# Post-norm transformer, two layers: two tiles of the second sequence's probabilities turned by squares instead of on TensorE, and the output bias added in another order

## The chip, the cores and the metric

The kernel runs on one core of a Trainium2 chip. The metric is the device time of one execution in microseconds (us); smaller is better. A core has a matrix engine (TensorE, PE in the profile; its weight loads are PEld), a vector engine (VectorE, DVE), a scalar engine (ScalarE, ACT), GpSimd (POOL) and SyncE (SP), which only issues transfers. They run side by side, each in its own instruction order, and wait for one another by semaphores. SBUF is the on-chip memory; PSUM holds the eight accumulators into which PE writes.

## The reference

Two sequences `b` of 512 tokens with 512 features go through two layers, each an attention and a feed-forward network, with a layer norm after every one of the four:

```python
x = _layernorm(x + _L0_attn_ref(x, ...))   # memory M and normaliser z instead of scores
x = _layernorm(x + _L0_ffn_ref(x, ...))    # ternary weights, int8 in between
x = _layernorm(x + _L1_attn_ref(x, ...))   # softmax(q k^T / sqrt(128)) v, one head, times Wo, plus bo
x = _layernorm(x + _L1_ffn_ref(x, ...))    # silu(x Wg^T) * (x Wu^T), times Wd^T
```

What the change touches is the memory read of the first attention (`num / den` for 8 heads, projected by `Wo`, summed over heads), the test that the first network's weights are ternary, and in the second attention

```python
attn = softmax(q k^T * scale);  out = attn @ v;  return out @ Wo + bo
```

## The kernel before, in words

All work is in tiles of 128 tokens (four a sequence, `NT`) or in blocks of 128 features (four, `NK`). GpSimd executes in the order of the program (L62). For the other engines a scheduler chooses the order; `tc.issue_after(step)` holds an instruction's place behind another's, and the small class `Chain` (L1275 on, `in_turn`) ties a list of steps into a row.

**First attention, reading the memory (L584 to L623, loop at L710).** M and Wo are folded into one 128x512 matrix a head, `mw`, the last column of which gives `den`. For each of eight token tiles `read(b, t)` does eight products `po` on PE (L593), one a head, into a PSUM tile each. ScalarE copies the column `den` (L597), VectorE takes its reciprocal, four heads at a time (L601). The first three heads (`LENT`) are scaled by ScalarE into `y` (L606) and summed on GpSimd (L610, and L622 into the tile `x`); the other five are multiplied and added into `x` by VectorE straight from PSUM (L615), the `steps` of the diff. The layer norm of one tile runs while the next one is read. A tile's PSUM accumulators come free when ScalarE or VectorE has read them.

**The checks (L625, `check_up`).** The first network's gate and up weights come in 11 chunks `gus`, two halves each. For each half ScalarE scales the weights to units (`t`), and VectorE compares that, scaled back, with the weights and counts what differs (`compare`, L211; the count is read out by a small second instruction). Eight of the 22 compares are popped from the list `checks` before the reading starts; the loop at L710 pops six more, two each behind tiles 0 and 1, one each behind 2 and 3, tied to the last fold (`folded`) alone, and the rest follow in the first network. Their sum `tot_up` (L217) and `verdict` follow at tiles 3 and 4.

**Second attention (loop over `b` at L1147, then L1185 to L1310).** Per sequence: queries and keys `pqk` (L1163), values `pv` (L1181), scores `psc` (L1117, PSUM, one 128x512 tile a token tile), the row maximum on VectorE (`maxima`, L1123, a reduction and a small multiplication), and the exponential with its row sum on ScalarE (`exponentials`, L1129). The product with the values needs the probabilities turned (keys on partitions). There are two ways in the kernel:

- on PE: `transposed` (L118) makes sixteen 128x128 transposes into four PSUM tiles and copies each to SBUF (ScalarE and VectorE take turns, L130). The second sequence's probabilities (`pt_p1`, copied to `xt_p1`) are turned so.
- by squares: VectorE turns every 32x32 square of a tile in place of its own (`nc.vector.transpose`, L1195), and `move_squares` (L301) moves the squares to their blocks. With `queues=3`, the default, it issues eight transfers on SyncE and four on GpSimd and leaves four to VectorE as copies (L320); with `queues=2` eight on SyncE and eight on GpSimd. The first sequence's probabilities (`squares_p0`, `pt0`) are turned so.

The output bias `bo` is added to the residual tiles `xs` ahead of time. For the first sequence GpSimd does it in four additions (L1196), in the loop that turns its squares; for the second, GpSimd issues four transfers that add while they write (L1211), behind a small copy `landed` that reads `pt0` (L1209) and so waits until that has been moved. Then `values` (L1221) multiplies values and turned probabilities (`pot`), `output` (L1243) multiplies by Wo (`po1`), `attended` (L1248, the row of L1250) divides by the row sum and adds the residual on VectorE, and `norm_a1` (L1254) normalises: statistics on VectorE, two small steps on GpSimd (L146, L1240), the application on ScalarE (L1241). The first sequence goes through this first, then three tiles of the second; then `turn_rows` (L1286, `pt_f`) turns the first sequence's rows on PE, and the fourth tile of the second sequence follows inside a `Chain`.

**Weights of the second network.** PE multiplies fp32 by parts in a faster format: `split_up` (L1063) cuts a chunk of weights into parts, ScalarE the upper one (`upper`, L1033) and VectorE two more (L1043, L1044), in gaps of the second attention. `table(func, behind)` (L1092) loads ScalarE's table of a function ahead of its first use with a one-element activation; the Silu table is loaded behind the last exponential of the second sequence. The network itself (`up1`, L1353 and L1398; down L1353) follows and takes the rest of the time.

Of the kernel before, what the change touches and what calls it, by code (L numbers as in the profile page):

```python
# [10 lines left out]
F32 = mybir.dt.float32  # L11
# [8 lines left out]
P = 128  # L20
# [19 lines left out]
def kernel(  # L40
# [285 lines left out]
    def pair_tile(name, dtype=F32):  # L326
        return wop.tile([P, 2, HID], dtype, tag="wo", name=name)
# [78 lines left out]
    with tc.tile_pool(name="a0w", bufs=1) as a0w, tc.tile_pool(name="a0", bufs=2) as a0:  # L406
# [303 lines left out]
        for i, (b, t) in enumerate(order):  # L710
            steps = read(b, t, lambda steps: norm_a0(i - 1, steps) if i else None)

            with tc.issue_after(folded.ins):
                for _ in range((2, 2, 1, 1)[i] if i < NT else 0):
                    check_up(*checks.pop(0))
            if i == 3:
                tot_up = total(counts_up[0], "up")
            elif i == 4:
                flag_up, eff_up = verdict(tot_up, sc_up, "up")
            if i == 1:  # L720
                squares0 = xtp.tile([P, NT, HID], F32, tag="xt", name="squares_0")
                xt0 = xtp.tile([P, NT, NK, P], F32, tag="xt", name="xt_f00")
            if 1 <= i <= TURNED:
                turn_squares(i - 1, squares0)
            if i == TURNED:
                move_squares(squares0[:, :TURNED], xt0[:, :TURNED], queues=1)
            if i == NT:
                parts, part, turned = split_tiles(0)
                x2.append(parts)
                part(TURNED, turned(TURNED))  # L730
            elif i == NT + 1:
                squares = xtp.tile([P, NT, HID], F32, tag="xt", name="squares")
                part(NT - 1, turned(NT - 1))
            if NT + 1 <= i <= NT + TURNED:
                with tc.issue_after(steps[0].ins):
                    part(i - NT - 1, xt0[:, i - NT - 1])
            if NT < i < len(order) - 1:
                turn_squares(i - 1, squares)
# [387 lines left out]

        return got, maxima

    def exponentials(b, got, behind={}):  # L1129
        sums = small.tile([P, NT], F32, tag="sums", name=f"sums_{b}")  # L1130
        row = []
        for t, (p, mx) in enumerate(got):
            if t % 2 == 0:
                two = pair_tile(f"prob_{b}_{t}")
            e = two[:, t % 2, :]
            with ExitStack() as tied:
                if t in behind:
                    tied.enter_context(tc.issue_after(behind[t].ins))
                moved = nc.scalar.activation(
                    e, p, AF.Exp, bias=mx, scale=scale, accum_out=sums[:, t : t + 1]  # L1140
                )
            row.append(e)
        probs.append((row, sums))
        return moved

    qkv = []
    for b in range(B):  # L1147
        if b:
            with tc.issue_after(copies[-2].ins), tc.issue_after(copies[-1].ins):
                split_up(0, room0)  # L1150
                split_up(1, room1[:6])
        qk = []
        qk2 = query_tile(f"qk_{b}")
        if b == 0:
            v2 = query_tile("v")
        pqk = [psum(f"pqk_{b}_{j}") for j in range(2)]
        xt = [xt_a11[:, :TURNED], xt_a11[:, TURNED:]] if b else xt_a10
        for half in (1, 0) if b else (0, 1):
            for j in range(2):
                for k in range(NK):  # L1160
                    p = pqk[j].rearrange("p (h t i) -> p h t i", h=2, i=P)[:, half]
                    rows = xt[half][:, :, k, :]
                    nc.tensor.matmul(  # L1163
                        p, wqkv[:, k, ts(j, D)], rows,
                        start=(k == 0), stop=(k == NK - 1),
                    )
        for j, p in enumerate(pqk):
            s = qk2[:, j, :]
            moved = nc.scalar.activation(s, p, AF.Identity, bias=bqk[:, j : j + 1])
            qk.append(s)  # L1170
        if b:
            pt0 = fp.tile([P, NT, NK, P], F32, tag="it10", name="pt_p0", bufs=1)
            move_squares(squares, pt0)
            pt0 = pt0.rearrange("p t k i -> p k t i")
        else:
            table(AF.Exp, moved)
        v = v2[:, b, :].rearrange("p (t d) -> p t d", t=NT)
        for t in range(NT):
            p = psum(f"pv_{b}_{t}")
            for k in range(NK):  # L1180
                nc.tensor.matmul(  # L1181
                    p[:, :D],
                    xt[t // TURNED][:, t % TURNED, k, :],
                    wqkv[:, k, ts(2, D)],
                    start=(k == 0), stop=(k == NK - 1),  # L1185
                )
            nc.vector.tensor_add(v[:, t, :], bv, p[:, :D])
        qkv.append((qk[0], qk[1], v))
        if b == 0:
            got, maxima = scores(0, turn_others)  # L1190
            maxima(range(NT))
            exponentials(0, got)
            squares = fp.tile([P, NT, HID], F32, tag="it00", name="squares_p0", bufs=1)
            for t in range(NT):
                nc.vector.transpose(squares[:, t, :], probs[0][0][t])  # L1195
                nc.gpsimd.tensor_add(xs[0][t], xs[0][t], bo)  # L1196


    room2 = room1[6:] + take(4)
# [2 lines left out]
            weight_upper(gus[turn[2]][:, a].rearrange("p k i -> p (k i)"), room2[3 * a])  # L1202

    got, maxima = scores(1)
    scaled_max = maxima(range(NT))
    table(AF.Silu, exponentials(1, got))

    landed = small.tile([P, 1], F32, tag="off", name="landed")
    nc.gpsimd.tensor_copy(landed[2 * SQ : 3 * SQ], pt0[2 * SQ : 3 * SQ, NK - 1, NT - 1, P - 1 :])  # L1209
    for t in range(NT):  # L1210
        nc.gpsimd.dma_start(xs[1][t], bo_in.to_broadcast([P, HID]), accum_op=ALU.add)  # L1211
    with tc.issue_after(scaled_max.ins):
        done = split_up(2, room2, True)
    with tc.issue_after(done.ins):
# [6 lines left out]
    def values(b, pt, cuts):  # L1221

        ot = ot2[:, b, :]
        w = S // cuts
        for i in range(cuts):
            po = psum(f"pot_{b}_{i}")
            for k in range(NT):
                nc.tensor.matmul(  # L1228
                    po[:, :w].rearrange("p (t i) -> p t i", i=P), qkv[b][2][:, k, :],
                    pt[:, k, ts(i, NT // cuts)],  # L1230
                    start=(k == 0), stop=(k == NT - 1),
                )
            (nc.vector.tensor_copy if b else nc.scalar.copy)(ot[:, ts(i, w)], po[:, :w])
        ots.append(ot)
# [8 lines left out]
    def output(b, t):  # L1243
        p = psum(f"po1_{b}_{t}")
        nc.tensor.matmul(p, ots[b][:, ts(t, P)], wo1, start=True, stop=True)  # L1245
        return p
# [52 lines left out]
        return pts, turned  # L1299

    values(0, pt0, 1)
    pt1 = transposed(probs[1][0], "p1").rearrange("p k (t i) -> p k t i", t=NT)
    for t in range(NT):
        attended(0, t, output(0, t))
        norm_a1(0, t)
    values(1, pt1, 2)
    for t in range(NT - 1):
        done = attended(1, t, output(1, t))
    rooms = [rows_room(0, "r0"), None]
    x3 = [row_blocks(rooms[0]), None]  # L1310
    pts, turned = turn_rows(0)
    with tc.issue_after(turned.ins):
        p = output(1, NT - 1)
    in_turn = Chain(done)
    for pt, (h, m, _) in zip(pts, x3[0]):
        in_turn(lambda: upper_lower(pt, h, m)[1])
    for t in range(NT - 1):
        in_turn(lambda: norm_a1(1, t))
    in_turn(lambda: attended(1, NT - 1, p))
    x = xs[1][NT - 1]  # L1320
    stats = layernorm_stats(x, f"a11_{NT - 1}")
    in_turn.last = taken[f"a11_{NT - 1}"]
    squares = xtp.tile([P, NT, HID], F32, tag="xt", name="squares_r1")
    for t in range(NT - 1):
        in_turn(lambda: nc.vector.transpose(squares[:, t, :], xs[1][t]))
    in_turn(lambda: layernorm_apply(x, x, stats))
    in_turn(lambda: nc.vector.transpose(squares[:, NT - 1, :], x))
    for h, m, d in x3[0]:
        in_turn(lambda: crossed(d, h, m))
    xt_r1 = fp.tile([P, NT, NK, P], F32, tag="it10", name="xt_f11", bufs=1)  # L1330
# [233 lines left out]
    for i, (b, j) in enumerate(steps):  # L1564
# [6 lines left out]
            while len(held) > 1:  # L1571
                moved = finish_up()
        if i == 1:
            in_turn(lambda: split_up(AHEAD - 1, take(6)))
        elif i == 2:
            rooms[1] = rows_room(1, "r1")
            x3[1] = row_blocks(rooms[1])
            for k in range(NK):
                with tc.issue_after(in_turn.last.ins):
                    uppers, in_turn.last = rows_from_squares(k)  # L1580

            landed = small.tile([P, 1], F32, tag="off", name="landed_r1")
            nc.gpsimd.tensor_copy(landed[:SQ], x3[1][NK - 1][0][:SQ, S - 1 :].bitcast(F32))
            gus[2:6] = up_weights(gu1_in, "1", range(2, 6), nc.gpsimd)
            wds = down_weights(wd1_in, "1", nc.gpsimd)
        elif i == AHEAD:
            for h, m, d in x3[1]:
                in_turn(lambda: crossed(d, h, m))
# [85 lines left out]
```

## Time and profile before

| what | value |
| --- | --- |
| time, median of 3 runs | 453.56 us (452.8 to 453.66) |
| the profiled execution's own time | 453.97 us |
| its span, first to last instruction | 452.2 us |
| mean granted TensorE clock | 0.999 |
| instructions | 5904 |
| packets of transfers, bytes | 37220, 38.97 MB |
| sixteen engines for transfers, share of the span used by the hardware queue / the software queue | 18.5% / 10.9% |
| memory read of the first attention, `po` L593, 128 PE records | 57.2 us busy, 599 ns each |
| VectorE's sums of it, L615, 40 | 29.8 us, 746 ns each |
| GpSimd's sums of `y`, L610, 16 | 21.3 us, 1332 ns each |
| the sixteen transposes of the second sequence's probabilities on PE, L128 | records of 273 ns that overlap, starting from 254.7 to 256.3 |

The page gives, for each engine, how long it was busy and what share of the span that is; then the span in 40 slices; the queues of the transfers; the chain of work that ended last, followed back from the end; and the costliest groups of instructions, each with its line, engine, operation, the tile that it writes and those that it reads, the count, the busy time, and the idle time just before with what ended it. In a timeline of an engine a row is: start in us, busy us, engine, line, operation, tiles, shapes, count, and in brackets how long the engine had idled before and which instruction it then followed ("0.50 <-PE pt_p L128"). Equal instructions that follow one another stand in one row, with the sum of their time.

### The profile page before, as it was taken

How to read it: one execution, taken by the hardware profiler on the slowest of the kernel's cores; microseconds unless marked ns; L12 is line 12 of the kernel's file. 1: busy time of each engine (PE TensorE's matmuls, PEld its weight loads, DVE VectorE, ACT ScalarE, POOL GpSimd, SP SyncE). 2: the span in 40 equal slices, each digit the busy share in tenths (PEclk: the TensorE clock that was granted, in tenths of full speed). 3: DMA queues.
4: the chain of work that ended last, by engine and by line, in shares of the span. 5: the costliest groups of instructions: out<-in, count | busy, mean ns of one | idle time of the engine just before them, and what ended most of it. 6: DMA issues, size and time to landing. Idle time of an engine off the chain costs nothing.

```text
span 452.2 us, 5904 instructions
## 1 busy us (share of the span) xinstructions
PE 444.8 (98%) x1921; PEld 338.9 (75%) x1921; DVE 317.7 (70%) x638; ACT 259.6 (57%) x494; POOL 127.8 (28%) x184
## 2 busy tenths in 40 slices
PE   8999999999999999999999999999999999999995
PEld 8887753444587888888878578888888888888885
DVE  4976657877886798858899999545535446777523
ACT  5788986467566975557745645454645446442311
POOL 0200205566650049302465347350000000011211
PEclk9999999999999999999999999999999999999999
DMA  8999990020028101121216603390000000000001
GB/s 297 396 268 318 169 331 6 0 44 7 1 46 238 42 2 48 48 94 39 34 33 160 101 1 53 83 393 3 0 1 0 1 2 0 1 18 29 34 37 70
DMA packets 37220, 38.97 MB, mean 86 GB/s; under 512 B 25264, under 2 KB 26160, under 8 KB 37184
## 3 DMA queue, kind: packets, MB, share of 16 engines
q1 hardware_dynamic: 32960, 26.66, 18.5%
q0 software_dynamic: 3936, 11.47, 10.9%
q8 instruction: 22, 0.36, 0.3%
q10 hardware_dynamic: 288, 0.36, 0.2%
q14 instruction: 14, 0.11, 0.1%
HBM read 32.45 MB, written 2.10 MB: 76 GB/s over the span
## 4 chain that ended last, share of the span: by engine, by line
PE 95%; ACT 2%; DMA 1%; DVE 1%; issue 0%; DVEq 0%; ACTq 0%
PE pu L1353 24%; PE pd L1353 13%; PE po L593 10%; PE pg_f L789 9%; PE pq L538 9%; PE pu_f L789 9%; PE pd_f L848 4%; PE pqk L1163 3%; PE pu L1398 2%; PE pv L1181 2%; PE pot L1228 2%; PE psc L1117 2%; PE po L1245 2%; DMA gu<-in_gu 1%; PE pmw L579 1%; PE pq L509 1%
## 5 line engine op out<-in xcount | busy, mean ns | idle before, releaser
L593 PE MATMUL po<-mw,q 128*128 128x512 f32 x128 | 57.2, 599 | 0.7 <-ACT y L606 0.6
L146 POOL TENSOR_TENSOR rstd_f<-mv_f,ln_eps 128x1 f32<-128x1 f32 x15 | 6.4, 428 | 163.2 <-DVE mv_f L1521 128.1
L1353 PE MATMUL pu<-r,ugu 128*128 128x512 f32 x200 | 48.6, 389 | 0.0
L364 ACT ACTIVATE pu<-pu 128x512 f32<-128x512 f32 x42 | 24.2, 581 | 41.3 <-PE pu L1353 37.6
L593 PEld LDWEIGHTS po<-mw,q 128*128 128x128 f32 x128 | 22.7, 189 | 33.6 <-issue 17.2
L1353 PEld LDWEIGHTS pu<-r,ugu 128*128 128x128 f32 x200 | 37.5, 188 | 7.8
L615 DVE SCALAR_TENSOR_TENSOR x<-po,den,x 128x511 f32<-128x511 f32 x40 | 29.8, 746 | 1.9
L170 ACT ACTIVATE ta_f<-y_f,below_half 128x512 int8<-128x512 f32 (+1 forms) x22 | 15.9, 722 | 24.6 <-DVE y_f L158 22.2
L610 POOL TENSOR_TENSOR y<-y,y 128x511 f32<-128x511 f32 x16 | 21.3, 1332 | 24.0 <-DVE x L615 20.3
L1412 DVE TENSOR_TENSOR it_f<-ev,pu 128x512 f32<-128x512 f32 x20 | 13.7, 685 | 16.0 <-PE pu L1353 15.6
L1353 PE MATMUL pu<-r,it_early 128*128 128x512 f32 x104 | 24.9, 389 | 0.0
L1241 ACT ACTIVATE x<-x,off_f,rstd_f 128x512 f32<-128x512 f32 x7 | 5.7, 815 | 32.0 <-POOL off_f L1240 32.0
L815 DVE SCALAR_TENSOR_TENSOR it_f<-tb_f,ta_f 128x512 fp32r<-128x512 int16 (+1 forms) x22 | 15.6, 707 | 11.1 <-ACT tb_f L171 11.1
L1353 PEld LDWEIGHTS pu<-r,it_early 128*128 128x128 f32 x104 | 19.5, 188 | 4.1
L1353 PE MATMUL pd<-ugu,r 128*128 128x512 f32 (+1 forms) x79 | 22.5, 362 | 0.0
L789 PE MATMUL pg_f<-x,tu 128*128 128x512 f32 x88 | 22.1, 393 | 0.0
L789 PE MATMUL pu_f<-x,tu 128*128 128x512 f32 x88 | 21.7, 389 | 0.0
L376 POOL TENSOR_SCALAR td<-wd,inv_down 128x512 fp32r<-128x512 f32 x11 | 19.9, 1824 | 3.2 <-DVE inv_down L206 3.2
L848 PE MATMUL pd_f<-td,it_f 128*128 128x512 f32 x88 | 20.3, 389 | 0.0
L597 ACT ACTIVATE den<-po,den_eps 128x1 f32<-128x1 f32 x64 | 14.0, 270 | 10.6 <-PE po L593 10.5
L789 PEld LDWEIGHTS pg_f<-x,tu 128*128 128x128 f32 x88 | 16.4, 188 | 4.0 <-DVE x L615 0.4
L789 PEld LDWEIGHTS pu_f<-x,tu 128*128 128x128 f32 x88 | 16.5, 188 | 3.4
(400 smaller groups left out, 1129.3 us busy)
## 6 DMA issues: line engine op xcount, KB each, us to landing
gu<-in_gu SPq DMA_DIRECT2D x16, 512.0 KB, 5.3
wo<-in_wo SPq DMA_DIRECT2D x8, 512.0 KB, 9.5
wo<-in_wo POOLq DMA_DIRECT2D x8, 512.0 KB, 9.1
wd<-in_wd SPq DMA_DIRECT2D x10, 256.0 KB, 5.4
wd<-in_wd POOLq DMA_DIRECT2D x10, 256.0 KB, 6.6
wq<-in_wq SPq DMA_DIRECT2D x8, 256.0 KB, 4.7
gu<-in_gu POOLq DMA_DIRECT2D x4, 512.0 KB, 5.1
x<-in_x SPq DMA_DIRECT2D x7, 256.0 KB, 4.3
```

The lines of the kernel that those rows point to most:

```text
L170: nc.scalar.activation(a[:n], y, AF.Relu, bias=below_half[:n])
L364: return nc.scalar.activation(p, p, AF.Copy, scale=BIG + 1.0)
L376: eng.tensor_scalar(out, w, factor, None, ALU.mult)
L538: done = nc.tensor.matmul(p, w, x, start=(start and i == 0), stop=(i == len(todo) - 1), skip_group_check=not start,)
L593: nc.tensor.matmul(po, qs[b][h0 + j][:, ts(t, P)], mw[:, h0 + j, :], start=True, stop=True,)
L597: nc.scalar.activation(den[:, j : j + 1], po[:, LAST:], AF.Identity, bias=den_eps)
L610: nc.gpsimd.tensor_add(ys[0][:, :LAST], ys[0][:, :LAST], y[:, :LAST])
L615: steps.append(nc.vector.scalar_tensor_tensor(x[:, :LAST], four[j][:, :LAST], d, x[:, :LAST], ALU.mult, ALU.add))
L789: nc.tensor.matmul(pp[a], t[:, a, i % NK, :], x2[b][i], start=(i == 0), stop=(i == 2 * NK - 1),)
L815: nc.vector.scalar_tensor_tensor(it[:n], tb[:n], 128.0, ta[:n], ALU.min, ALU.subtract)
L848: nc.tensor.matmul(pd, inter[b][c][:, ts(t, P)], td[c].bitcast(F32R), start=(c == 0), stop=(c == last),)
L1353: done = nc.tensor.matmul(p, w, x, start=(start and i == 0), stop=(i == n - 1), skip_group_check=not start,)
```

## The change

Three edits.

1. The late checks are tied to the first VectorE sum of the tile behind which they are popped, besides the last fold.
2. Of the second sequence's probabilities tiles 0 and 1 (`TURNED` = 2) are turned by squares, with eight transfers on SyncE and eight on GpSimd, each half as large as with four tiles; tiles 2 and 3 stay on PE, eight transposes instead of sixteen, now into a PSUM tile per token tile. VectorE's turns stand between the maxima, and the exponentials are split accordingly. The product `pot` of the second sequence takes its halves in reverse order, the token tiles that come last in the chain are chosen so that tile 1 is the last instead of tile 3, and the Silu table load and a later weight split are tied behind the copy of tile 2.
3. The bias transfers to the second sequence's residual tiles take the place of the additions in the first sequence's loop, and the additions for the first sequence stand where the transfers were, ahead of the eight transfers that GpSimd issues for edit 2. The copy `landed` is gone.

```diff
@@ loop at L710
-            with tc.issue_after(folded.ins):
+            with tc.issue_after(folded.ins), tc.issue_after(steps[0].ins):
                 for _ in range((2, 2, 1, 1)[i] if i < NT else 0):
                     check_up(*checks.pop(0))
@@ exponentials, L1129
-    def exponentials(b, got, behind={}):
...
+    def exponentials(b, got, tiles=range(NT)):
+        if 0 in tiles:
+            pairs = [pair_tile(f"prob_{b}_{t}") for t in range(0, NT, 2)]
+            sums = small.tile([P, NT], F32, tag="sums", name=f"sums_{b}")
+            probs.append(([u for two in pairs for u in units(two)], sums))
+        row, sums = probs[b]
+        for t in tiles:
+            p, mx = got[t]
+            moved = nc.scalar.activation(
+                row[t], p, AF.Exp, bias=mx, scale=scale, accum_out=sums[:, t : t + 1]
+            )
         return moved
@@ loop over b, b == 0, L1194
             for t in range(NT):
                 nc.vector.transpose(squares[:, t, :], probs[0][0][t])
-                nc.gpsimd.tensor_add(xs[0][t], xs[0][t], bo)
+                nc.gpsimd.dma_start(xs[1][t], bo_in.to_broadcast([P, HID]), accum_op=ALU.add)
@@ behind the loop, L1204
     got, maxima = scores(1)
-    scaled_max = maxima(range(NT))
-    table(AF.Silu, exponentials(1, got))
-
-    landed = small.tile([P, 1], F32, tag="off", name="landed")
-    nc.gpsimd.tensor_copy(landed[2 * SQ : 3 * SQ], pt0[2 * SQ : 3 * SQ, NK - 1, NT - 1, P - 1 :])
+    squares1 = fp.tile([P, NT, HID], F32, tag="it00", name="squares_p1", bufs=1)
+    pt1 = xtp.tile([P, NT, NK, P], F32, tag="xt", name="xt_p1")
+    scaled_max = maxima(range(TURNED))
+    exponentials(1, got, range(TURNED))
+    for t in range(TURNED):
+        turned = nc.vector.transpose(squares1[:, t, :], probs[1][0][t])
+        with tc.issue_after(turned.ins):
+            scaled_max = maxima([TURNED + t])
+        exponentials(1, got, [TURNED + t])
     for t in range(NT):
-        nc.gpsimd.dma_start(xs[1][t], bo_in.to_broadcast([P, HID]), accum_op=ALU.add)
+        nc.gpsimd.tensor_add(xs[0][t], xs[0][t], bo)
+    move_squares(squares1[:, :TURNED], pt1[:, :TURNED], queues=2)
     with tc.issue_after(scaled_max.ins):
         done = split_up(2, room2, True)
@@ values
-        for i in range(cuts):
+        for i in reversed(range(cuts)):
@@ behind values(0, pt0, 1)
-    pt1 = transposed(probs[1][0], "p1").rearrange("p k (t i) -> p k t i", t=NT)
+    for t in range(TURNED, NT):
+        pt = psum(f"pt_p1_{t}")
+        for k in range(NK):
+            nc.tensor.transpose(pt[:, ts(k, P)], probs[1][0][t][:, ts(k, P)], ident)
+        move = nc.vector.tensor_copy if t % 2 else nc.scalar.copy
+        moved = move(pt1[:, t], pt.rearrange("p (k i) -> p k i", k=NK))
+        if t % 2 == 0:
+            table(AF.Silu, moved)
+            settled = moved
+    pt1 = pt1.rearrange("p t k i -> p k t i")
...
-    for t in range(NT - 1):
+
+    *others, final = [*range(TURNED, NT), *range(TURNED)]
+    for t in others:
         done = attended(1, t, output(1, t))
...
@@ second network, steps
         if i == 1:
-            in_turn(lambda: split_up(AHEAD - 1, take(6)))
+            with tc.issue_after(settled.ins):
+                in_turn(lambda: split_up(AHEAD - 1, take(6)))
```

Where the diff is cut behind `others`, every `range(NT - 1)` of the old text has become `others` and every `NT - 1` has become `final`.

More of the change, by code (lines that the diff above doesn't have):

```diff
@@ L1127, in scores @@
         return got, maxima
-    def exponentials(b, got, behind={}):
[L1130 to L1143, printed above, removed]
+    def exponentials(b, got, tiles=range(NT)):
[9 more added lines that the diff above has]
+            )
         return moved
@@ L1312 @@
     with tc.issue_after(turned.ins):
-        p = output(1, NT - 1)
+        p = output(1, final)
     in_turn = Chain(done)
@@ L1316 @@
         in_turn(lambda: upper_lower(pt, h, m)[1])
-    for t in range(NT - 1):
+    for t in others:
         in_turn(lambda: norm_a1(1, t))
[L1319 to L1322, printed above, removed]
+    in_turn(lambda: attended(1, final, p))
+    x = xs[1][final]
+    stats = layernorm_stats(x, f"a11_{final}")
+    in_turn.last = taken[f"a11_{final}"]
     squares = xtp.tile([P, NT, HID], F32, tag="xt", name="squares_r1")
-    for t in range(NT - 1):
+    for t in others:
         in_turn(lambda: nc.vector.transpose(squares[:, t, :], xs[1][t]))
     in_turn(lambda: layernorm_apply(x, x, stats))
-    in_turn(lambda: nc.vector.transpose(squares[:, NT - 1, :], x))
+    in_turn(lambda: nc.vector.transpose(squares[:, final, :], x))
     for h, m, d in x3[0]:
```

## The prediction

> **What bounds the kernel now.** I read the page's busy rows and chain of waits first, then the chain in order of time, then the timelines of the two stages that the diff touches.
>
> ```profile
> span 452.2 us, 5904 instructions
> PE 444.8 (98%) x1921; PEld 338.9 (75%) x1921; DVE 317.7 (70%) x638; ACT 259.6 (57%) x494; POOL 127.8 (28%) x184
> ...
> PE 95%; ACT 2%; DMA 1%; DVE 1%; issue 0%; DVEq 0%; ACTq 0%
> ```
>
> PE ends last nearly everywhere, so an edit counts only by how far it moves PE. The chain in order of time leaves PE in one long stretch, 59.32 to 73.24, where the reading of the first token tile starts; from there to 446.86 it is PE alone. But PE without idle time can still be paced: an operand that is ready just in time is invisible in the chain, and becomes the limit when it moves. I therefore follow VectorE (DVE) too.
>
> **Edit 1, the late checks (L713).** Six compares (L211) stood ahead of the first tile's sums; now two stand behind the first sum of tile 0, two in tile 1, one each in tiles 2 and 3. VectorE's timeline:
>
> ```profile
> 70.68 1.56 DVE L211 SCALAR_TENSOR_TENSOR junk<-t,sc_up,gu 128x512 int8<-128x512 f32 x1
> 72.17 0.08 DVE L211 DVE_READ_ACCUMULATOR junk<-t,sc_up,gu 128x1 f32 x1
> 72.17 0.17 DVE L601 RECIPROCAL den<-den 128x4 f32<-128x4 f32 x1
> 72.28 0.17 DVE L217 TENSOR_REDUCE tot_up<-counts 128x1 f32<-128x14 f32 x1
> 72.44 3.31 DVE L615 SCALAR_TENSOR_TENSOR x<-po,den,x 128x511 f32<-128x511 f32 x4
> 75.67 0.17 DVE L601 RECIPROCAL den<-den 128x4 f32<-128x4 f32 x1
> 75.94 0.75 DVE L615 SCALAR_TENSOR_TENSOR x<-po,den,x 128x511 f32<-128x511 f32 x1
> 78.37 0.18 DVE L601 RECIPROCAL den<-den 128x4 f32<-128x4 f32 x1 [1.68 <-ACT den L597]
> ```
>
> The reciprocal at 72.17 waited behind a compare. Its last input came from ScalarE at 71.09 (70.79 + 0.30), and in the new order of ScalarE I count it to 70.95. So the four sums move up about 1.1 us and free PSUM for PE that much sooner. What is late next: the two compares of tile 1 (0.75 each and 0.08 for reading the count, 1.66) go into the hole of 1.68 before 78.37. They would just fit, but GpSimd's additions (L622, L610, 1.27 each) run there, and 70.68 above shows what that does: 1.56 instead of 0.75 beside such an addition. With sums 1.1 earlier, L622 runs from 74.75 and L610 from 76.13; the first compare, due at 75.47, waits to 75.88, the second to about 77.6, and the reciprocal comes at 78.33 instead of 78.37. The gain is then given back to 0.04. Nothing restores it: the sums of a tile, the reciprocal, ScalarE's three scaled copies and the next sums form a loop of 7.3 us a tile (sums end at 82.36 and 89.69), against 6.9 of PE. The compares of tiles 2 and 3 have holes of 1.62 and 1.47 for 0.83. Bounds 0 to 1.1; I take **-0.2**, near the blocked row.
>
> **Edit 2, two tiles turned in squares.** PE does 8 transposes fewer: 16 take 1.75 in the chain, so -0.88. The copy of `ot` (L1233) stood behind the Silu table load, its warm-up and an `ugu` copy (1.28 + 0.20 + 0.61) and started at 255.42; with those moved behind it, it can start when pot ends (254.83), so PE's next product (po, 256.42) can come at about 255.7. But VectorE carries the next step. Timeline now:
>
> ```profile
> 249.44 0.69 DVE L1123 TENSOR_REDUCE mx<-psc 128x1 f32<-128x512 f32 x1
> ...
> 255.75 0.69 DVE L130 COPY xt_p<-pt_p 128x512 f32<-128x512 f32 x1 [0.50 <-PE pt_p L128]
> 256.62 0.69 DVE L130 COPY xt_p<-pt_p 128x512 f32<-128x512 f32 x1 [0.18 <-PE pt_p L128]
> 257.55 0.75 DVE L1250 SCALAR_TENSOR_TENSOR x<-po,sums,x 128x512 f32<-128x512 f32 x1 [0.23 <-PE po L1245]
> ```
>
> Added between the maxima: two turns (0.71 and 0.65 in the rows of L1195), 1.35 with the waits for their exponentials. Gone: one copy (0.69) and the idle 0.91. The first sum at 257.55 moves by -0.25. From there VectorE is dense to 263.93, and the fourth tile's norm ends on ScalarE at 266.06 (265.25 + 0.81); PE's first block of pt_f (265.88) takes that tile in its fourth transpose, so end of pt_f = that norm + 1.5 = 267.6, against 267.8 in the chain. **Slack 0.2: behind it, every us on VectorE is a us on PE.**
>
> The sixteen transfers of `xt_p`: SyncE issues eight at 0.66 and GpSimd eight at 0.6, 5.3 us from the second turn, and they land 1.9 later (row xt_a). The turn ends at 253.1 without delays, so 260.3; the reversed halves use them last, after four po and half of pot, at 260.9 by my count. Hidden, by 0.6; the issues on GpSimd also end before its first norm step (now 259.92). On SyncE nothing waits behind.
>
> **Edit 3, bias transfers and sums change places.** This is the term that decides. GpSimd now adds from 245.68 to about 250.6, just behind its pt_p issues, where VectorE has, back to back:
>
> ```profile
> 243.09 2.57 POOL L316 DMA_DIRECT2D pt_p<-squares_p  x4 [2.07 <-DVE squares_p L1195]
> ...
> 245.70 0.68 DVE L1043 SCALAR_TENSOR_TENSOR it_early<-it_early,gu 128x512 fp32r<-128x512 f32 x1
> 246.30 0.41 DVE L320 COPY pt_p<-squares_p 32x512 f32<-32x512 f32 x1
> 246.63 0.67 DVE L1044 TENSOR_TENSOR it_early<-it_early,it_early 128x512 fp32r<-128x512 f32 x1
> 247.32 1.29 DVE L320 COPY pt_p<-squares_p 32x512 f32<-32x512 f32 x3
> ```
>
> What an addition there does is seen where it stands today, and in the stages before:
>
> ```profile
> 236.06 4.97 POOL L1196 TENSOR_TENSOR x<-x,bo 128x512 f32<-128x512 f32 x4
> 240.49 1.09 DVE L1043 SCALAR_TENSOR_TENSOR it_early<-it_early,gu 128x512 fp32r<-128x512 f32 x1
> 98.53 0.94 DVE L233 TENSOR_SCALAR eff_up<-sc_up,yes_up,no_up 128x2 f32<-128x2 f32 x1
> 402.28 1.40 POOL L146 TENSOR_TENSOR rstd_f<-mv_f,ln_eps 128x1 f32<-128x1 f32 x1 [96.74 <-DVE mv_f L1521]
> ```
>
> L1043 took 1.09, not 0.68: it ran on only when the additions ended at 241.03. L233, with one SBUF tensor as input, took 0.94 (0.27 at 171.35). An L290 at 113.92 took 1.49, not 0.42, beside L610: 1.07 is what one addition costs whoever waits from its start. The turns (0.71) and the maxima (0.68, from PSUM) in the same stretch lost nothing, so only VectorE work from SBUF is hit. The last row is the other side: GpSimd's 0.19 waited 1.2 us through three VectorE operations, each issued before the one ahead ended. Without a gap VectorE mostly goes first; with one, the waiting addition does (69.98: between two compares). In the stretch above, the three copies from 247.32 stand 0.013 apart, issued after the one ahead has ended: three gaps, and a waiting addition each.
>
> No row shows a copy L320 beside an addition. Bounds: nothing, if VectorE keeps its turn; four additions, 4 x 1.07 = 4.3. Nearest are L233 (one SBUF input, blocked) and the gap at 69.98; I take three, 3 x 1.07 = 3.2. Less the 0.41 that L1043 loses today at 240.49: **+2.8 on VectorE**. The first sum moves by 2.8 - 0.25 = 2.55, pt_f by 2.55 - 0.2 = **+2.3 on PE**. PE's saved 0.88 is idle time then.
>
> The Trainium skill's "SBUF — State Buffer", section "SBUF: two separate sides", speaks against this edit: it calls the port pair shared by VectorE and GpSimd an exclusive lock, held for a whole instruction, and counts an fp32 copy from SBUF to SBUF among those that take it. The blocked rows agree. By its "whole instruction" four additions would cost 4 x 1.27 = 5.1 on VectorE and the sum would be 1.9 higher, an estimate; by rows for two-input operations alone it would be the first rival.
>
> The bias transfers (3.64 of issues at 250.26, 6.1 to land) start at 236.1 in place of the additions (4.97), so GpSimd is free before the turn at 242.8 as now; they are needed at 264.37. The `landed` copy (0.18) costs nothing. `settled`, the order of halves and of `final` keep all counts.
>
> **Sum** against the profiled execution: 453.97 (452.2 and 1.8 around it) - 0.2 + 2.3 = 456.1; it is 0.41 above the median of 453.56, so **455.7** on the median's footing.
>
> **Rivals.** (a) One addition gets in, in the idle port time between L1043 and L1044, and the copies pass: 1.07 - 0.41 - 0.25 - 0.2 = +0.2, less 0.2: 453.6. For it: no row has a copy blocked. (b) The other side: VectorE stays ahead of all four additions, as in the row of 402.28. VectorE gains 0.41 + 0.25, PE 0.86; with 0.2 to 1.1 of edit 1 that is 452.5 to 451.6, say 452.0. It decides from fewer than one addition before the maximum at 249.44. (c) The bias transfers, now with the gu loads (two of 512 KB at 236.9) and ahead of pt_p, make pt_p late: PE's pot (LDWEIGHTS at 250.81) and the first turn (it overwrites what pt_p reads) wait. The DMA row is busy some 7 us for the biases (252 to 259.5), 3.3 for gu, 4.3 for pt_p; one after another from 237.8 they end at 252.6, 1.5 late for the turn at 251.15: 454.4 without any blocking. Against it: pt_p is spread over 5 us by its issues anyway.
>
> **Chances.** Forecast 0.50, its own range 454.6 (two additions) to 456.8 (four); (a) 0.18; (b) 0.24; (c) 0.08. Faster by over 0.2% (0.9 us, about what a measurement tells from no change) is (b), 0.24; within it (a) and part of (c), 0.21; slower 0.55. The range 452.0 to 456.9 leaves out half of (b) and a tail above.
>
> **What would show it.** Right: rows of L320 and L1043 near 246 longer by about 1.1, the maximum of the second sequence 2 to 4 us later behind its pv, ScalarE's fourth norm as PE's releaser before pt_f, additions of 1.3 to 2 us; the reciprocal of tile 1 near 78.3. Wrong: L320 at 0.42 beside the additions; po straight behind eight transposes; pot waiting for a transfer, which is (c).

## The result, and the profile after

The changed kernel takes 458.56 us (median of 5 runs, 457.61 to 459.0) against 453.61 for the kernel before: a ratio of 1.0109, 95% interval 1.0097 to 1.012. It is 4.95 us slower; the forecast was 455.7, and the range up to 456.9 does not hold it. The profiled execution took 457.61.

From the page of the changed kernel, the counterpart of the rows shown of before:

```profile
span 455.8 us, 5910 instructions
PE 446.3 (98%) x1913; PEld 338.7 (74%) x1913; DVE 323.5 (71%) x639; ACT 259.4 (57%) x493; POOL 131.9 (29%) x191
...
PE 90%; DVE 7%; ACT 1%; issue 1%; POOL 0%; ACTq 0%; DVEq 0%; POOLq 0%
```

PE is still 98% busy, with eight instructions fewer. But VectorE now holds 7% of the chain that ended last, where it had 1%: a stretch in which PE follows VectorE. VectorE's timeline of the changed kernel shows where:

```profile
242.93 6.79 DVE L1044 TENSOR_TENSOR it_early<-it_early 128x512 fp32r<-128x512 f32 x2
...
250.24 0.41 DVE L320 COPY pt_p<-squares_p 32x512 f32<-32x512 f32 x1
...
253.37 0.68 DVE L1123 TENSOR_REDUCE mx<-psc 128x1 f32<-128x512 f32 x1
```

Before, the same two stood in VectorE's timeline as

```profile
244.50 1.28 DVE L1044 TENSOR_TENSOR it_early<-it_early 128x512 fp32r<-128x512 f32 x2
```

And GpSimd's, in the same stretch of the changed kernel:

```profile
241.53 2.67 POOL L316 DMA_DIRECT2D pt_p<-squares_p  x4 [2.97 <-DVE squares_p L1191]
244.22 4.95 POOL L1211 TENSOR_TENSOR x<-x,bo 128x512 f32<-128x512 f32 x4
```

Two L1044 took 6.79 instead of 1.28, 5.5 more, and they end 0.55 after the fourth addition: **one VectorE instruction, the second L1044 (6.19), waited for all four additions**. Everything behind it is as long as it was, the copies L320 too (0.41), and comes later. The first row maximum of the second sequence stands at 253.37, and PE, done with the scores, waits for VectorE to read the values out of a PSUM tile (L1183; waits of the changed kernel: us, times, longest):

```profile
PE pot L1229 <- DVE v L1183: 2.7, 1, 2.7
```

To compare kernels whose earlier stages differ by some tenths, I use one length from PE's timeline: from the end of the second sequence's `pv` to the end of `pt_f`. It is 19.82 in the kernel before and 24.66 in the changed one, +4.84, nearly the whole loss of 4.95.

### The profile page after: what moved, and what is told of

Same layout as the page of the kernel before. It is cut to its first block, busy times and chain, and to the rows that moved or that the text cites. A ratio compares the mean times of both kernels' runs of the same rounds, so it can differ in the third digit from the quotient of the medians.

```text
span 455.8 us, 5910 instructions
## 1 busy us (share of the span) xinstructions
PE 446.3 (98%) x1913; PEld 338.7 (74%) x1913; DVE 323.5 (71%) x639; ACT 259.4 (57%) x493; POOL 131.9 (29%) x191
## 4 chain that ended last, share of the span: by engine, by line
PE 90%; DVE 7%; ACT 1%; issue 1%; POOL 0%; ACTq 0%; DVEq 0%; POOLq 0%
PE pu L1365 23%; PE pd L1365 13%; PE po L593 12%; PE pq L538 9%; PE pg_f L789 9%; PE pu_f L789 9%; PE pd_f L848 4%; DVE it_early L1044 2%; PE pu L1410 2%; PE po L1246 2%; PE pmw L579 2%; PE pq L509 1%; PE pot L1229 1%; PE ph L1365 1%; PE rise L113 1%; PE pdc L1365 1%
## 5 line engine op out<-in xcount | busy, mean ns | idle before, releaser
L146 POOL TENSOR_TENSOR rstd_f<-mv_f,ln_eps 128x1 f32<-128x1 f32 x15 | 5.4, 359 | 163.9 <-DVE mv_f L1533 128.8
L848 PEld LDWEIGHTS pd_f<-td,it_f 128*128 128x128 f32 x88 | 16.5, 188 | 3.4
```

Of the source, the lines that this page charges most:

```text
L848: nc.tensor.matmul(pd, inter[b][c][:, ts(t, P)], td[c].bitcast(F32R), start=(c == 0), stop=(c == last),)
```

## The experiments

Theory: the loss is VectorE held up by the four additions, for their whole row. Rivals: the transfers (the bias ahead of `pt_p`, or `xt_p` by itself) do it, and the additions only cover that; or an addition slows VectorE wherever it stands. Each kernel is compared with runs of the kernel before on the same chip.

| kernel | median us | ratio to before, 95% | end of pv to end of pt_f |
| --- | --- | --- | --- |
| before | 453.6 to 454.1 | | 19.82 |
| edit 1 alone | 453.52 | 0.9999 (0.999 to 1.0008) | 19.83 |
| edit 3 undone | 458.2 | 1.0103 (1.0084 to 1.0121) | 22.41 |
| edit 3 alone | 458.39 | 1.0104 (1.0089 to 1.0119) | 24.62 |
| sums by transfer | 461.17 | 1.0165 (1.0151 to 1.0179) | 27.99 |
| a pause behind each sum | 459.77 | 1.013 (1.0103 to 1.0156) | 24.93 |
| no sums | 453.62 | 0.9994 (0.9982 to 1.0006) | 19.74 |
| edit 2, no bias transfers | 453.29 | 0.9993 (0.9979 to 1.0007) | 20.47 |
| bias transfers last | 455.26 | 1.0049 (1.0026 to 1.0072) | 21.27 |
| sums beside the maxima | 454.08 | 1.0003 (0.9991 to 1.0015) | 20.31 |
| two sums | 455.97 | 1.0038 (1.0024 to 1.0052) | 22.21 |

The last column is of the one profiled execution of each, the others of all runs (with the pauses, of three out of four).

**Edit 1 alone.** The kernel before with

```diff
-            with tc.issue_after(folded.ins):
+            with tc.issue_after(folded.ins), tc.issue_after(steps[0].ins):
```

> The kernel before with edit 1 alone. Theory from the trace of after: the six compares kept the first reciprocal, and behind it ScalarE's scaled copies, back by 1.9 us, PE stood idle for it, and nothing takes that back: 453.6 - 1.3 = 452.3. Rival, the step as recorded in the prediction: only the second reciprocal moves, and the compares of tile 1 give it back: 453.6 - 0.2 = 453.4.

Measured: 453.52. The interval is 0.45 below to 0.36 above the kernel before: my theory of 1.3 from the two profiles falls, and the prediction's 0.2 can't be told from nothing. The two profiles had the reading, from the first `po` to the first `pg_f`, at 58.32 before and 57.06 after, and PE's idle 0.57 and 0.17 in it gone. But edit 3 alone, which has the old order of the checks, needs 57.30, with no idle time of PE, and edit 1 alone 57.04. What was different in the profiled execution of before is one row of ScalarE's timeline:

```profile
65.14 0.72 ACT L374 ACTIVATE tu<-gu,inv_up 128x512 fp32r<-128x512 f32 x1 [0.92 <-DMA gu<-in_gu]
```

The same row in the kernel with edit 3 alone:

```profile
64.78 0.72 ACT L374 ACTIVATE tu<-gu,inv_up 128x512 fp32r<-128x512 f32 x1
```

In that execution of the kernel before the weights landed late under the reading, and the six compares could not start. It is not the only one: ScalarE waits 0.60, 0.51 and 0.21 for them in the profiles of two sums, of no sums and of the sums beside the maxima, which all have edit 1, and there the reading takes 57.76, 57.65 and 57.37. So late weights lengthen the reading in the new order as in the old; where they land in time, the two orders are 0.26 apart in one profile each. The profiled execution of the changed kernel also began its reading early, at 61.79, where the ten experiments begin at 62.1 to 62.6; that would account for most of the 0.95 that it took less than its median.

**Edit 3 undone** (edits 1 and 2 stay, and `landed` is back ahead of the second loop).

```diff
-                nc.gpsimd.dma_start(xs[1][t], bo_in.to_broadcast([P, HID]), accum_op=ALU.add)
+                nc.gpsimd.tensor_add(xs[0][t], xs[0][t], bo)
...
-        nc.gpsimd.tensor_add(xs[0][t], xs[0][t], bo)
+        nc.gpsimd.dma_start(xs[1][t], bo_in.to_broadcast([P, HID]), accum_op=ALU.add)
```

> After with edit 3 undone: the four additions in the first sequence's loop, the copy landed and the bias transfers ahead of the transfers of xt_p; edits 1 and 2 stay. Theory (all of the loss is the additions holding VectorE up): 453.6 - 1.3 (edit 1) - 0.45 (edit 2, the 0.25 and 0.2 of the prediction) = 451.9, and the parts of the weights at 243 to 250 run at 0.6 to 0.7 us each. Rival (turning two tiles by squares costs by itself, by the turns between the maxima or late transfers): above 454.

Measured: 458.2, with runs from 456.12 to 459.49, against a theory of 451.9. VectorE is free of waits, as the theory has it (two L1044 in 1.28), yet the time is not won. GpSimd's timeline, and then the waits, of this kernel:

```profile
249.83 3.65 POOL L1213 DMA_DIRECT2D x<-in_bo  x4 [0.33 <-issue]
253.32 3.69 POOL L316 DMA_DIRECT2D xt_p<-squares_p  x6
```

```profile
PE pot L1231 <- DMA xt_p<-squares_p: 3.1, 1, 3.1
```

The bias transfers are issued ahead of `xt_p` and are in flight beside them; those of `xt_p` take 6.0 us to land, not 1.9 to 2.6 as in the kernels where no bias transfer is beside them, and GpSimd's last two issues wait 1.10 and 1.43 for a bias transfer. So edits 2 and 3 hang together: with the old places of the bias, edit 2 costs some 4.6; with the new ones, the additions cost 4.9. The profile explains 2.6 of the 4.6 (22.41 against 19.82): it is of the fastest of the six runs, and what the others wait for is open.

**Edit 3 alone.** The kernel before with the bias transfers in the first sequence's loop, the additions behind `scores(1)`, and no `landed`.

> The kernel before with edit 3 alone. Theory: the four additions, one behind another without a gap, hold VectorE up for their whole time, 5.5 us for one L1044, less 0.4 saved, less 0.2 of slack: 453.6 + 4.9 = 458.5. Rival 1, the recorded step (three of four additions get in, 1.07 each): 456.2. Rival 2 (the loss needs the turns and transfers of edit 2): 453.6.

Measured: 458.39, the theory's 458.5. VectorE's timeline:

```profile
243.73 6.78 DVE L1044 TENSOR_TENSOR it_early<-it_early 128x512 fp32r<-128x512 f32 x2
```

The two L1044 take as long without edit 2, to 0.01 us.

**Sums by transfer.** The changed kernel with

```diff
-        nc.gpsimd.tensor_add(xs[0][t], xs[0][t], bo)
+        nc.gpsimd.dma_start(xs[0][t], bo_in.to_broadcast([P, HID]), accum_op=ALU.add)
```

> After, with the four additions on GpSimd replaced by four accumulating transfers of the bias in the same place. Theory (the shared port): no VectorE operation is stretched, 451.9 as with edit 3 undone. Rival (the bias transfers, early or many, delay the transfers of the probabilities): above 455, with pot waiting for a transfer.

Measured: 461.17, against a theory of 451.9. No VectorE row is stretched, but the rival's mechanism is there in full:

```profile
PE pot L1229 <- DMA pt_p<-squares_p: 5.8, 1, 5.8
```

Eight bias transfers around `pt_p` hold it up until 256.7. This kernel therefore says nothing on the additions; it shows that the transfers are a second brake as soon as there are more of them.

**No sums.** The changed kernel without the four additions.

```diff
-        nc.gpsimd.tensor_add(xs[0][t], xs[0][t], bo)
```

> After without the four additions: the first sequence's output bias is left out; the bias transfers of the second stay where they are. Theory (the additions carry the loss; the early bias transfers let the transfers of pt_p land at about 250 to 251, some 1 us later than before but just in time): 453.6 - 0.45 + 0.2 = 453.3. Rival 1 (the early bias transfers are a second brake of the same size behind the additions): 455 to 457, with pot or the first turn of the second sequence waiting for pt_p. Rival 2 (the transfers of xt_p come late once nothing else is): 455 to 457, with the second product pot waiting for xt_p.

Measured: 453.62, the time of before. The additions carry the loss. The transfers of `pt_p` take 5.5 us to land in the changed kernel (2.4 on SyncE's queue and 2.8 on GpSimd's before), but without the additions `pot` starts at 251.40, 0.33 behind the last score, and the length to the end of `pt_f` is 19.74: the delay is hidden. The two L1044 take 1.28 again, beside the same four issues of GpSimd.

**Two sums.** The changed kernel with additions for two tiles.

```diff
-    for t in range(NT):
+    for t in range(2):
         nc.gpsimd.tensor_add(xs[0][t], xs[0][t], bo)
```

> After with two of the four additions (the output bias of two tiles of the first sequence is left out). Theory (VectorE waits from 0.6 us ahead of the first addition to the end of the last, whatever their number): L1044 takes about 3.7 us instead of 6.2, the time lies half way between none (453.6) and four (458.6), at 456.1 to 456.4. Rival (the loss is a threshold: it comes only when PE runs idle for so long that its clock falls): 454 or less, or 458 and more.

Measured: 455.97, a little under the theory's 456.1: 1.9 more than before, and in the profile 2.47 more than with none (22.21 against 19.74), half of the 4.92 for four. VectorE's timeline:

```profile
243.99 4.35 DVE L1044 TENSOR_TENSOR it_early<-it_early 128x512 fp32r<-128x512 f32 x2
```

4.35 - 1.28 = 3.07 for a row of additions of 2.51; with four it was 5.51 for 4.95. Both times the wait is the row's length and 0.56.

**A pause behind each sum.** The changed kernel with

```diff
         nc.gpsimd.tensor_add(xs[0][t], xs[0][t], bo)
+        pause = small.tile([P, 1], F32, tag="off", name=f"pause_{t}")
+        nc.gpsimd.tensor_copy(pause[:1], xs[0][t][:1, :1])
```

> After, with a one-element copy on GpSimd behind each of the four additions, which reads what the addition wrote, so that no two additions follow one another without a pause. Theory A (whichever engine holds the port keeps it as long as its instructions follow one another without a pause): VectorE gets in behind the first addition, L1044 takes about 2 us instead of 6.2; the other three additions come in at the pauses between the copies of L320, and the time stays between 456.5 and 458.6. Rival B (GpSimd goes first whatever stands between): L1044 over 6 us, 458.6 or more.

Measured: 459.77, the median of 458.49, 459.77 and 460.06; one execution of 1173.77 is left aside, and its cause is not known. VectorE's timeline, then GpSimd's:

```profile
243.55 3.13 DVE L1044 TENSOR_TENSOR it_early<-it_early 128x512 fp32r<-128x512 f32 x2
246.60 1.89 DVE L1043 SCALAR_TENSOR_TENSOR it_early<-it_early,gu 128x512 fp32r<-128x512 f32 x1
248.41 1.62 DVE L320 COPY pt_p<-squares_p 32x512 f32<-32x512 f32 x1
```

```profile
244.84 1.28 POOL L1211 TENSOR_TENSOR x<-x,bo 128x512 f32<-128x512 f32 x1
246.18 0.54 POOL L1213 COPY pause<-x 1x1 f32<-1x1 f32 x1
```

At each pause VectorE gets one instruction in (the second L1044 takes 2.53 and ends at 246.67, beside the small copy), and then it waits for the next addition: 1.85, 1.21, 1.21 and 1.12 (the three L320, 2.40 for 1.28), 5.39 in all. Half of theory A holds: a row of additions without a pause gives nothing away, a pause does. The other half falls: VectorE's own row without a pause was broken: from the second L1044 on, four of five instructions waited. The copies L320 from SBUF to SBUF wait as well, 1.62 and 1.53 instead of 0.41. The sum in the profile stays the same. Rival B falls on L1044, for which it had over 6 us, though the time lies in its range; that the other two runs took 1.3 to 1.6 more than the profiled one is not explained.

**Edit 2 without bias transfers** (edits 1 and 2, additions in the loop as before).

> Edits 1 and 2 with the additions in the first sequence's loop as before and without any bias transfer: the second sequence's output bias is left out. Prices edit 2 without its neighbours. The prediction's step: 453.6 - 0.45 - 0 (edit 1 alone measured at nothing) = 453.1, xt_p landing at about 260 and pot not waiting for it. Rival (the sixteen transfers of xt_p are late by themselves): above 454.5, with pot waiting for xt_p.

Measured: 453.29 against 453.70 for before, no difference that the interval shows. The first sum on VectorE comes at 256.88, 0.29 earlier than with edit 1 alone. In the profile PE waits 1.1 for `xt_p`; but that execution took 454.17, 0.88 more than the median. In the profiles of no sums, of the bias transfers last and of the sums beside the maxima PE does not wait for `xt_p`: the cover holds mostly, not always.

**Bias transfers last** (as the one before, with the transfers issued behind those of `xt_p`).

> Edits 1 and 2, additions in the first sequence's loop as before, and the bias transfers of the second sequence issued behind those of xt_p, in the order in which the tiles are used. Theory: xt_p is alone on the transfer engines until about 260, the bias lands from 262 to 267, in time but for the last tiles: 453.1 to 454.2. Rival (the sums of the second sequence wait for their bias): 455 or more, with a wait of attended for x.

Measured: 455.26. `xt_p` is in time, but four more issues on GpSimd hold the norms behind them: ScalarE's first norm starts at 262.70 instead of 260.40, and `pt_f` waits for the last. The rival's wait for the bias is there too, 0.71 ahead of one sum (L1251 at 265.41), but the chain that ended last runs through the queue of GpSimd, which neither theory had. The profile is of the fastest of ten runs, which go up to 459.08.

**Sums beside the maxima.** The changed kernel with the additions behind the first maximum of the second sequence.

```diff
+    behind = small.tile([P, 1], F32, tag="off", name="behind")
+    nc.gpsimd.tensor_copy(behind, got[0][1])
     for t in range(NT):
         nc.gpsimd.tensor_add(xs[0][t], xs[0][t], bo)
```

> After, with a one-column copy on GpSimd ahead of the four additions that reads the second sequence's first row maximum, so that the additions run from about 250 to 255, beside VectorE's maxima (from PSUM) and turns. Theory (only VectorE work with its tensors in SBUF is held up; the place of the additions decides): the maxima and turns keep 0.65 to 0.71 us, the L1043 behind them (253.8) waits about 1.1, the transfers of xt_p start 1.7 later and pot waits for them by about 1: 454.6 to 455.6. Rival (additions on GpSimd hold VectorE up wherever they stand): 457.5 or more, with maxima of 1 us and longer.

Measured: 454.08 against 454.10 for before, better than expected. GpSimd's row, then VectorE's:

```profile
249.89 4.95 POOL L1213 TENSOR_TENSOR x<-x,bo 128x512 f32<-128x512 f32 x4
```

```profile
249.60 0.68 DVE L1123 TENSOR_REDUCE mx<-psc 128x1 f32<-128x512 f32 x1
...
252.03 0.65 DVE L1123 TENSOR_REDUCE mx<-psc 128x1 f32<-128x512 f32 x1
252.61 0.69 DVE L1206 STREAM_TRANSPOSE squares_p<-prob 128x512 f32<-128x512 f32 x1
...
254.04 1.35 DVE L1043 SCALAR_TENSOR_TENSOR it_early<-it_early,gu 128x512 fp32r<-128x512 f32 x1
```

The same four additions, as long as before, cost nothing beside maxima and turns; the one L1043 that starts under them waits 0.67. The place decides, and these two lines take back the whole loss. No kernel tried is measurably faster than the one before.

## Why the prediction was wrong, step by step

The direction, the stretch and the edit were right: edit 3, VectorE behind the issues of `pt_p`, PE late by what VectorE is late. The sum was 2.9 too small: 2.3 of that is one term, 0.2 the slack, and up to 0.2 edit 1.

- **The step that failed: "I take three, 3 x 1.07 = 3.2", and its upper bound, "four additions, 4 x 1.07 = 4.3".** Measured: 5.5, one wait for all four. The price came from rows where an addition was followed by a pause, and so did the picture that a waiting VectorE instruction gets in between two additions: the two additions at 69.98 depend on one another, and the second starts 0.08 after the first has ended (71.76 and 71.68). The four of edit 3 do not; each starts before the record of the one ahead ends (245.45 and 245.50), and the wait is their whole row. That row's length stood in the very view that I showed, 4.97 for four. The bound from above should have been this, the whole row of additions and not four times one wait. The number, three, came from the gaps between VectorE's copies, which the additions never met.
- The Trainium skill's "SBUF — State Buffer", section "SBUF: two separate sides", speaks of a lock for a whole instruction; the 5.1 that the prediction worked out from it is nearer to the measured 5.5 than my own 3.2. What the runs add is that nothing is given away between additions either, unless there is a pause.
- "Without a gap VectorE mostly goes first": wrong for this stretch. In the kernel with pauses four of five VectorE instructions in a row let an addition pass.
- The copies L320, of which I expected the waits, ran at 0.41 to 0.42: the additions were over when they came. The rows that I named as the sign (L320 and L1043 longer by 1.1) did not appear; one L1044 had it all. Nor did the additions wait for VectorE: they took 1.26 to 1.28 each, where I had 1.3 to 2. The first maximum of the second sequence did come later behind its `pv`, by 5.1, where I had 2 to 4.
- **From VectorE to PE**: +5.5, less 0.41, less 0.25 is +4.84, and the length from `pv` to the end of `pt_f` grew by 4.84. So the slack of 0.2 that I took off is not there. The rule behind it, "end of pt_f = that norm + 1.5", was mis-sized: the end of `pt_f` stands 1.73 behind the fourth norm in the kernel before (267.79 and 266.06), and 1.69 in the changed kernel and without sums.
- **Edit 1, -0.2**: measured 0.0, with 0.45 less to 0.36 more in the interval, so its size is open. That compares in the hole of tile 1 are blocked was right (1.11 and 1.63 instead of 0.75); the wait that edit 1 was to remove belonged to executions with late weights.
- **Edit 2**: the first sum earlier by 0.29 (forecast 0.25). "Hidden, by 0.6" for `xt_p` held in most profiles; it failed by 1.1 in one where nothing else was late, and by 3.1 beside the bias transfers.
- **Rival (c)**: its mechanism is there, 5.5 instead of 2.4 to 2.8 for `pt_p` to land, and is hidden; with four transfers more it costs 5.8 us of waiting. Rival (b) did not come; the kernel without additions has VectorE as free as (b) has it, but takes 453.62 and not 452.0.

That GpSimd's additions and VectorE's two-input work from SBUF exclude one another is shown by the runs with none, two, four and elsewhere placed. Why the wait is 0.56 longer than the row of additions is open; the issue of the last transfer just ahead of them does not do it alone, since the same L1044 ran in 0.69 beside it in the kernel with the sums beside the maxima.

## What to carry to other kernels

Before moving work to GpSimd, list what VectorE does in that stretch from SBUF, with two inputs or as a copy: here it waited for the whole unbroken row of GpSimd additions, not for one of them. Where VectorE reads PSUM or turns squares, the same additions were free. And compare a stage in the profiles of several kernels that share it before pricing a wait in it: the one that edit 1 was to remove came from weights that landed late, in four of twelve profiled executions, with edit 1 and without.

## What was not expected of the hardware

Windows of the changed kernel (busy time of PE, PEld, VectorE, ScalarE, GpSimd with their counts; then the granted clock, the transfers' share and GB/s), where PE had stood idle for 2.68 us from 250.24:

```profile
252.00:253.00 1.00, 0.08 (x1) 0.08 (x1) 0.96 (x5) 0.00 (x0) 0.00 (x0) 1.00 0.00 0
254.00:255.00 1.00, 1.00 (x2) 0.34 (x1) 0.93 (x4) 0.72 (x2) 0.00 (x0) 0.50 0.00 0
```

The clock fell to 0.50 after the idle time, when PE was at work again, and the eight `pot` took 5.4 us instead of 3.6. Edit 3 alone shows the same after 2.66 us of idle time. In the kernel with pauses, with 2.54 us of idle time, it stayed at 1.00, and `pot` took 3.7. It cost nothing that shows: with the pauses PE had the faster clock and then waited 1.7 for a probability, and both stages are about equally long (24.66 and 24.93).
